# A graph attention layer with gathered rows: other PSUM banks for three intermediate results, masks fetched first, and a clearing behind each gather

## The chip, the cores and the metric

The kernel runs on one core of one Trainium2 chip. The metric is the device time of one execution in microseconds (us); the median of several runs is what counts. Engines are named as in the profile: PE does the matrix products (PEld its weight loads), DVE is the vector engine, ACT the scalar engine, POOL is GpSimd, SP the engine that here only starts transfers. PSUM is the memory that PE writes to, divided into banks; SBUF is the memory that all engines share.

## The reference

There are 3125 nodes with 128 features (`x`), and 100000 edges with a source, a destination and one of five types. The edges are sorted by destination. For each type r, and eight heads of 16 features:

```python
mask = edge_types == r
q = jnp.einsum('eh,khd->ekd', x_dst, W_Q[r])
k = jnp.einsum('eh,khd->ekd', x_src, W_K[r])
v = jnp.einsum('eh,khd->ekd', x_src, W_V[r])
logits = (q * k).sum(-1) / scale + attn_bias[r][None, :]
masked_logits = jnp.where(mask[:, None], logits, NEG)
max_v = jax.ops.segment_max(masked_logits, dst, num_segments=n)
max_v = jnp.maximum(max_v, NEG)
exp_l = jnp.where(mask[:, None], jnp.exp(masked_logits - max_v[dst]), 0.0)
sum_exp = jax.ops.segment_sum(exp_l, dst, num_segments=n)
attn = exp_l / (sum_exp[dst] + 1e-12)
out = out + jax.ops.segment_sum(attn[:, :, None] * v, dst, num_segments=n)
```

So it is a softmax over the edges of one type that end in one node, and a weighted sum of values. The sum over types is projected, `x` is added and a layer norm taken; the kernel's output is the layer norm of `x` plus that.

## The kernel before

The edges are cut into 196 groups of 512 (`GE`), a group into 4 tiles of 128 (`T`). They are worked off in 66 steps (`NST`): the first has one group, all others three, so twelve tiles.

*Prologue.* Up to about 132 us the kernel multiplies all nodes with the weights of all types and stores rows of keys and values in a table in device memory (`kv_d`, from the lines 522 and 525), prepares keys and masks of the edges and the first blocks of query rows (`q_d`), and checks its input. Its SBUF tiles are given back (`pre.close()`), and the pool `flow`, from which the loop takes its tiles, lies in that space.

*Gathers.* Each tile of 128 edges needs 128 rows of the table. `gather` (line 865) fetches them by an indirect transfer that POOL starts, one for each tile, 719 in all. They go into four places that are used in turn, two in `kv_early` and two in `kv_late`. `point(k, j, leave)` stands at eleven places of a step; each lets the gathers go that are due by then, two steps ahead (`KV_LEAD`), behind the instruction `leave` (`behind`, line 150, adds that as a wait). One tile of each of 63 steps is not gathered but computed (the "early" tile): `early_places` makes a 0/1 matrix on ACT (lines 1046, 1047), `early_turn` selects columns of `x` with it on PE (1052, into `lt`), `early_turned` copies them to `xr` on ACT (1056), `early_rows` multiplies them with the weights on PE (1063), and `early_keep` copies the rows to their place on ACT (1070).

*One step k*, in the order of the program (`for k in range(NST)`; each engine runs its own instructions in this order, and waits where data or a bank is not free):

- places of one group on ACT (1132, 1136): 0/1 matrices that later sum edges into nodes;
- `products` on DVE (958): queries, spread to the edges, times gathered keys; `logits` (999) sums them over the features of a head into `spare`; `closed_lanes` (973) adds a mask of types; `turn_logits` (1031) transposes them on PE into `lt`;
- `norm` of step k-2 on DVE (1168 to 1172), `relations` (1188, PE: the sum over types, called rows by node) and `by_node` (1192, ACT: copies them to their place among the nodes);
- `spread_q` on PE (938): spreads the queries of step k+1 to its edges, into `qe`; `queries` (896, PE) and `first_part`, `remainder`, `second_part`, `third_part` (901 to 914, ACT and DVE) make query rows of later blocks, in three parts of bf16, and `store_q` stores them;
- `weigh` of step k-1 on DVE (1119): values times weights; `sums` on PE (1146, 1151) for the three groups of step k-1, into `both`, with other work between;
- `scans` on DVE (1076, 1079): the running maximum within a node, from `lt` and masks (`mk`) that a transfer brought; `less_max` (1088, DVE), `exps` (1096, ACT), `turn_exps` (1103, PE, into `mid`), `weights` (1113, ACT, a copy out of `mid`);
- `take(k)` on SP: starts the transfers for later steps, first the keys (`fetch_keys`, 741) and twelve sets of query rows (`fetch_rows`, 764), then the masks (`fetch_masks`, 924).

Blocks of 128 nodes that are complete are projected, normed and stored between these (`project` and others).

*PSUM.* Eight banks are in use: `mid` (one bank), `qe` (three), `lt` (two), `both` (one) and one under the tag `fin`. Waits between engines arise by bank within a tile: an instruction that writes a bank waits for those that still read it. Before the change, `mid` holds the weights of the edges, `spare`, and what is projected; `qe` is taken anew for spread queries and for the rows of the x tile in turn; `both` holds sums, denominators and the rows by node; `fin` holds query rows.

Of the kernel before, what the change touches and what calls it, by code (L numbers as in the profile page):

```python
# [18 lines left out]
P = 128  # L19
# [123 lines left out]
def windowed_path(  # L143
# [684 lines left out]
    ps = ctx.enter_context(tc.tile_pool(name="ps", bufs=1, space=PSUM))  # L828
    late = kv_tile("kv_late", KVB - KVA)
    mid = ps.tile([P, 4 * P], F32, name="mid")  # L830
    flow = ctx.enter_context(tc.tile_pool(name="flow", bufs=2))

    def place(k):
# [23 lines left out]
        for k in range(NST)  # L857
    ]
    issued = []

    def gather(leave=None, n=1):
        for q in sum(tiles, [])[len(issued) :][: max(n, 0)]:
            ((kv, at, _),) = runs(q, q + 1)
            behind(
                nc.gpsimd.indirect_dma_start(  # L865
                    out=kv[:, at, :], out_offset=None, in_=kv_d[:, :],
                    in_offset=bass.IndirectOffsetOnAxis(
                        ap=idx[:, q % T, q // T : q // T + 1], axis=0
                    ),
                ),  # L870
                leave,
            )
            issued.append(q)

    def point(k, j, leave):
        at = k + (j + 1) / POINTS + KV_LEAD
# [15 lines left out]
    def queries(b, c0, c1):  # L892
        if c0 == 0:
            live["q3", b] = flow.tile([P, R, 3, H], BF16, name="q3", bufs=2)
        pr = ps.tile([P, c1 - c0, H], F32, name="prq", tag="fin")
        nc.tensor.matmul(pr, live["xT", b], wq[:, c0:c1, :], start=True, stop=True)  # L896
        live["pr", b, c0] = pr, live["q3", b][:, c0:c1], c1 - c0

# [21 lines left out]
    def fetch_masks(k):  # L920
        n = len(groups(k))
        live["mk", k] = mk = flow.tile([L3, MW], BF16, name="mk", bufs=2)
        rows = msk_d[G0[k] : G0[k] + n]
        nc.sync.dma_start(
            mk[: n * LANES, :],
            bass.AP(tensor=rows.tensor, offset=rows.offset, ap=[[MW, n], [0, LANES], [1, MW]]),
        )

    def spread_q(k):
        hot, qw = live.pop(("hot", k)), live.pop(("qw", k))  # L930
        n = B0[k + 1] - B0[k]
        live["qe", k] = qe = ps.tile([P, T * G3, H], F32, name="qe")
        dest = [qe[:, j, :] for j in range(min(n, T * G3))]
        if k == 0:
            live["qe0"] = qe0 = ps.tile([P, H], F32, name="qe0", tag="fin")
            dest = [qe0] + dest
        for j in range(n):
            spread = nc.tensor.matmul(  # L938
                dest[j], hot[:, j * P : (j + 1) * P], qw[:, j, :], start=True, stop=True
            )  # L940
        return spread
# [3 lines left out]

    def products(k):
        a, b = B0[k], B0[k + 1]
        qe = live.pop(("qe", k))
        if k == 0:
            ((kv, c0, c1),) = runs(0, 1)  # L950
            nc.vector.tensor_tensor(
                kv[:, c0, :H], kv[:, c0, :H], live.pop("qe0"), op=ALU.mult
            )
            a = 1
        n = 0
        for kv, c0, c1 in runs(a, b):
            m = n + c1 - c0
            made = nc.vector.tensor_tensor(
                kv[:, c0:c1, :H], kv[:, c0:c1, :H], qe[:, n:m], op=ALU.mult
            )  # L960
            n = m
        return made
# [3 lines left out]
            live["lx", k] = flow.tile([P, T * (G3 + 1), R, HEADS], F32, name="lx", bufs=2)  # L966
        return live["lx", k]

    spare = mid[:, 2 * P : 2 * P + (T * G3 + 1) * HEADS].rearrange("p (t k) -> p t k", k=HEADS)

    def closed(a, lg, q0):
        n, m = lg.shape[1], a.shape[1]
# [84 lines left out]

    def early_rows(k):
        xr = live.pop("xr")
        qe = ps.tile([P, T * G3, H], F32, name="qe")  # L1060
        live["rows"] = rows = qe[:, :2, :].rearrange("p s h -> p (s h)")
        for r in range(R):
            nc.tensor.matmul(  # L1063
                rows, xr[:, r * P : (r + 1) * P], wkv[:, r].rearrange("h s c -> h (s c)"),
                start=(r == 0), stop=(r == R - 1),
            )

    def early_keep(k):
        ((kv, c0, _),) = runs(B0[k + 1] - 1, B0[k + 1])
        nc.scalar.copy(kv[:, c0, :], live.pop("rows"))  # L1070
# [86 lines left out]
    def both(k):  # L1157
        if ("both", k) not in live:
            live["both", k] = ps.tile([P, G3 * (PW + HEADS + WN)], F32, name="both")
        return live["both", k]  # L1160
# [18 lines left out]
        live.pop(("both", k))  # L1179
        return begun, ended  # L1180

    def relations(k, room=None):
        o5 = live.pop(("o5", k))
        if room is None:
            room = both(k + 1)[:, G3 * (PW + HEADS) :]
        live["nodes", k] = nodes = room[:, : G3 * WN].rearrange("p (g w) -> p g w", g=G3)
        for i, g in enumerate(groups(k)):
            nc.tensor.matmul(nodes[:, i], o5[:, i], rsum[:WR], start=True, stop=True)  # L1188
# [150 lines left out]
    fetch_rows(2)  # L1339

    def take(k):
        if k + 3 < NST:
            fetch_keys(k + 3)
            fetch_rows(k + 3)
        if k + 2 < NST:
            fetch_masks(k + 2)

    def half(k):
        if k - 1 in q_at:
# [4 lines left out]
    for k in range(NST):  # L1354
        new, old = k >= 1, k >= 2
        q0, (q, c0, c1), (q1, d0, _) = q_at.get(k), half(k), half(k - 1)
        done, rooted = block_at.get(k), block_at.get(k - 1)
        place_g, sum_g = list(groups(k - 1)), list(groups(k - 1))

        def place_next():  # L1360
            return places(place_g.pop(0)) if place_g else None

        def sum_next():
            if sum_g:
                sums(sum_g.pop(0))

        soon, near = k + 2 in early_at, k + 1 in early_at
        if q1 is not None:
            second_part(q1, d0)
        if near:  # L1370
            early_turned(lt)
        place_next()
        if soon:
            early_places(k + 2)
        if k == NST - 2:
            places(G0[k + 1])
        elif k == NST - 1:
# [24 lines left out]
        point(k, 0, weigh(k - 1) if new else kept)  # L1402
        point(k, 1, kept)
        pass_on(k)
        if q is not None:
            first_part(q, c0)
        place_next()
        if k == NST - 1:
            place_next()
        sum_next()  # L1410
        for j, leave in enumerate(scans(k)):
            point(k, 2 + j, leave)
        if k == done_at[begun]:
            project(begun)
        if done is not None:
            project(done)
        sum_next()
        lt = live["lt", k]
        less_max(k)
        exps(k)  # L1420
        if q0 is not None:
            turn_q(q0)
            turned(q0)
        placed = place_next() if k < NST - 1 else None
        if k == NST - 1:
            places(G0[k] + 2)
        if k + 2 < NST:
            point(k, 4, spot(k + 2))
        point(k, 5, placed)
        if done is not None:  # L1430
            shifted(done)
            residual(done)
        if k == NST - 1:
            for b in range(NT - len(ends), NT):
                lifted(b)
            for b in range(begun, NT):
                shifted(b)
# [23 lines left out]
    room = ps.tile([P, T * G3, H], F32, name="qe").rearrange("p n h -> p (n h)")  # L1461
    fin = ps.tile([P, RH * H], F32, name="prq", tag="fin")
    live["both", k] = room[:, : G3 * (PW + HEADS + WN)]
    weights(k)
    roots(begun, last=True)
# [540 lines left out]
```

## Time and profile before

| | |
|---|---|
| median of 3 runs | 1312.44 us (1310.02 to 1320.14) |
| the profiled execution's own time | 1318.95 us |
| its span in the trace | 1317.2 us |
| PE / PEld busy | 1006.5 / 743.7 us |
| DVE busy | 904.5 us |
| ACT busy | 689.3 us |
| POOL busy | 797.9 us |
| mean granted clock of PE | 0.838 of full speed |

Times in the trace are microseconds from the span's start. A row of the timeline has the start, the duration, the engine, the line of the kernel, the operation, what is written and read, and in brackets how long the engine had been idle and which instruction ended that. "Remote" stands where the trace names no instruction that ended it, "issue" where the engine waited for nothing that the profile shows. The ends of matrix products are modelled. The chain is followed back from the last instruction, at each step to what released it. For the 719 gathers, the first began at 101.97 us and the last at 1276.74 us.

### The profile page before, as it was taken

How to read it: one execution, taken by the hardware profiler on the slowest of the kernel's cores; microseconds unless marked ns; L12 is line 12 of the kernel's file. 1: busy time of each engine (PE TensorE's matmuls, PEld its weight loads, DVE VectorE, ACT ScalarE, POOL GpSimd, SP SyncE). 2: the span in 40 equal slices, each digit the busy share in tenths (PEclk: the TensorE clock that was granted, in tenths of full speed). 3: DMA queues.
4: the chain of work that ended last, by engine and by line, in shares of the span. 5: the costliest groups of instructions: out<-in, count | busy, mean ns of one | idle time of the engine just before them, and what ended most of it. 6: DMA issues, size and time to landing. Idle time of an engine off the chain costs nothing.

```text
span 1317.2 us, 20087 instructions
## 1 busy us (share of the span) xinstructions
PE 1006.5 (76%) x5425; PEld 743.7 (56%) x5425; DVE 904.5 (69%) x1520; ACT 689.3 (52%) x1882; POOL 797.9 (61%) x793
## 2 busy tenths in 40 slices
PE   6984477988777877878788867777777877787776
PEld 3442355666565655656566655565555656566554
DVE  2545576768775777777776777686677677687776
ACT  1432255656565565546456646455555556465554
POOL 6664566666665666666665756665665566666650
PEclk9996679768888889888788888897888888878877
DMA  6884455555555555545555554555555455555440
GB/s 167 297 292 147 113 141 153 140 150 149 146 142 138 133 148 154 151 129 140 149 137 151 152 148 127 144 136 147 149 146 122 140 152 143 147 150 138 128 107 8
DMA packets 176110, 192.63 MB, mean 146 GB/s; under 512 B 121764, under 2 KB 137072, under 8 KB 175873
## 3 DMA queue, kind: packets, MB, share of 16 engines
q0 software_dynamic: 36528, 98.42, 28.4%
q1 hardware_dynamic: 138271, 91.97, 24.4%
q10 hardware_dynamic: 1194, 0.92, 0.3%
q8 instruction: 44, 0.72, 0.2%
q14 instruction: 73, 0.60, 0.2%
HBM read 160.80 MB, written 30.40 MB: 145 GB/s over the span
## 4 chain that ended last, share of the span: by engine, by line
PE 50%; DVE 16%; ACT 12%; another core or an unknown queue 11%; issue 9%; DMA 1%; SPq 1%; DVEq 0%; ACTq 0%
PE both L1151 14%; PE qe L1063 7%; PE lt L1052 5%; PE pr L522 5%; PE mid L1103 4%; ACT at L1132 4%; PE qe L938 3%; PE both L1146 3%; PE prq L896 2%; PE both L1188 2%; DVE wv L1119 2%; DVE mid L999 2%; DVE run L1076 2%; DVE run L1079 2%
## 5 line engine op out<-in xcount | busy, mean ns | idle before, releaser
L865 POOL DMA_INDIRECT kv_early<-kv_d,idx x366 | 372.2, 1017 | 217.6 <-issue 83.6
L865 POOL DMA_INDIRECT kv_late<-kv_d,idx x353 | 360.2, 1020 | 230.8 <-issue 70.0
L1151 PE MATMUL both<-wv,at 128*125 128x136 f32 x1544 | 326.3, 346 | 57.8 <-ACT oT L1192 24.8
L1151 PEld LDWEIGHTS both<-wv,at 128*125 128x125 f32 x1544 | 257.0, 230 | 142.9 <-issue 70.5
L1132 ACT ACTIVATE at<-wide_at,nkey 128x125 f32<-128x125 f32 x772 | 244.0, 391 | 0.0
L1063 PE MATMUL qe<-wkv,xr 128*128 128x256 f32 x630 | 162.4, 408 | 42.1 <-ACT xr L1056 24.7
L1076 DVE TENSOR_TENSOR_SCAN run<-mk,lt 120x640 f32<-120x640 bf16 (+1 forms) x66 | 97.8, 1482 | 105.6 <-remote 66.1
L1063 PEld LDWEIGHTS qe<-wkv,xr 128*128 128x128 f32 x630 | 124.0, 205 | 63.9 <-ACT xr L1056 27.9
L938 PE MATMUL qe<-qw,hot 120*128 120x128 bf16 x784 | 71.5, 257 | 76.8 <-ACT kv_late L1070 27.9
L1136 ACT ACTIVATE at<-at 128x500 f32<-128x500 f32 x193 | 119.6, 620 | 6.1
L938 PEld LDWEIGHTS <-hot 120*128 120x128 bf16 x784 | 66.7, 124 | 79.0 <-issue 78.4
L1188 PE MATMUL both<-rsum,o 125*128 125x25 f32 x380 | 59.7, 291 | 56.2 <-DVE o L1172 42.4
L1079 DVE TENSOR_TENSOR_SCAN run<-mk,run 120x640 f32<-120x640 bf16 (+1 forms) x66 | 98.5, 1492 | 2.3
L1052 PE MATMUL lt<-diag,xg 128*128 128x512 f32 x252 | 98.6, 520 | 0.0
L1103 PE MATMUL mid<-gather_heads,ls 120*128 120x24 f32 (+1 forms) x528 | 75.5, 283 | 22.6 <-ACT xTq L890 12.6
L999 DVE TENSOR_REDUCE mid<-kv_early 128x8 f32<-128x128 f32 (+3 forms) x51 | 61.3, 1202 | 45.6 <-ACT wv L1113 31.8
L1192 ACT COPY oT<-both 128x25 f32 x190 | 34.2, 180 | 111.4 <-PE both L1188 33.3
L1103 PEld LDWEIGHTS mid<-gather_heads,ls 120*128 120x128 f32 (+1 forms) x528 | 73.7, 215 | 29.6 <-ACT xTq L890 15.4
L1188 PEld LDWEIGHTS both<-rsum,o 125*128 125x128 f32 x380 | 53.6, 213 | 61.8 <-issue 56.5
L1146 PE MATMUL both<-wv,over 128*5 128x136 f32 x384 | 87.8, 316 | 0.0
L999 DVE TENSOR_REDUCE mid<-kv_late 128x8 f32<-128x128 f32 (+2 forms) x48 | 58.9, 1227 | 39.5 <-ACT wv L1113 29.1
L1168 DVE TENSOR_SCALAR both<-both 125x24 f32<-125x24 f32 (+1 forms) x65 | 12.1, 186 | 101.7 <-remote 49.2
(205 smaller groups left out, 1475.1 us busy)
## 6 DMA issues: line engine op xcount, KB each, us to landing
qw<-q_d SPq DMA_DIRECT2D x784, 30.0 KB
kt<-key_d SPq DMA_DIRECT2D x64, 360.0 KB
kv_d<-kvs SPq DMA_DIRECT2D x24, 640.0 KB
q_d<-q SPq DMA_DIRECT2D x25, 480.0 KB
mk<-msk_d SPq DMA_DIRECT2D x65, 150.2 KB
kv_early<-kv_d,idx POOLq DMA_INDIRECT x366
kv_late<-kv_d,idx POOLq DMA_INDIRECT x353
out<-z SPq DMA_DIRECT2D x24, 64.0 KB
```

The source lines that it names most:

```text
L865: nc.gpsimd.indirect_dma_start(out=kv[:, at, :], out_offset=None, in_=kv_d[:, :], in_offset=bass.IndirectOffsetOnAxis(ap=idx[:, q % T, q / ...
L938: spread = nc.tensor.matmul(dest[j], hot[:, j * P : (j + 1) * P], qw[:, j, :], start=True, stop=True)
L999: made = nc.vector.tensor_reduce(lg[:, n : n + c1 - c0], heads(kv[:, c0:c1, :H]), AX.X, ALU.add)
L1052: nc.tensor.matmul(lt[:, c0:c1], xg[:, e, :], at[:, c0:c1], start=True, stop=True)
L1063: nc.tensor.matmul(rows, xr[:, r * P : (r + 1) * P], wkv[:, r].rearrange("h s c -> h (s c)"), start=(r == 0), stop=(r == R - 1),)
L1076: there = nc.vector.tensor_tensor_scan(run[:n], mk[:n, :WIDE], lt, -BIG, op0=ALU.add, op1=ALU.max)
L1079: back = nc.vector.tensor_tensor_scan(run[:n, ::-1], mk[:n, WIDE:0:-1], run[:n, ::-1], -BIG, op0=ALU.add, op1=ALU.max)
L1103: nc.tensor.matmul(ex.rearrange("p (i t) k -> p t i k", t=T)[:, t], ls[: n * LANES, t * P : (t + 1) * P], gather_heads[: n * LANES, :n], s ...
L1132: nc.scalar.activation(at[:, t, :], row_at[:, :WR], AF.Abs, bias=nkey[:, t, g : g + 1], scale=1.0)
L1146: nc.tensor.matmul(pp[:R], over[:, g, :], live["wv", last][:, T * j + T - 1, :], start=False, stop=False,)
L1151: nc.tensor.matmul(pp[:WR], at[:, t, :], wv[:, T * i + t, :], start=(t == 0), stop=(t == end))
L1188: nc.tensor.matmul(nodes[:, i], o5[:, i], rsum[:WR], start=True, stop=True)
```

## The change

It has four parts.

1. *Banks.* `qe` (three banks) and `fin` (one) become tiles that are allocated once, as `mid` is. The sums over heads (`spare`) go from `mid` to the third bank of `qe`, behind the spread queries. The rows of the x tile (`early_rows`) go from a fresh `qe` to `mid`. The rows by node (`relations`) go from `both` to the end of `fin`, where the query rows are too.
2. *Order.* `early_rows` and `early_keep` stand right behind the first placement, ahead of `early_places` and the products. `third_part` and `store_q` stand ahead of `norm`. `queries` and `first_part` stand behind the first sums.
3. *Masks.* `take` starts the masks' transfer ahead of keys and query rows.
4. *Clearing.* A tile `idle` of 128 x 128 float32, which nothing reads, is taken from `flow`, and POOL clears it behind each gather. Beside it, the space reserved for the descriptors of such transfers is set to 8192 bytes.

```diff
     mid = ps.tile([P, 4 * P], F32, name="mid")
+    qe = ps.tile([P, T * G3, H], F32, name="qe")
+    fin = ps.tile([P, 4 * P], F32, name="fin")
...
+    idle = flow.tile([P, P], F32, name="idle", bufs=1)
...
             issued.append(q)
+            nc.gpsimd.memset(idle, 0.0)
...
-        pr = ps.tile([P, c1 - c0, H], F32, name="prq", tag="fin")
+        pr = fin[:, : (c1 - c0) * H].rearrange("p (c h) -> p c h", h=H)
...
-        live["qe", k] = qe = ps.tile([P, T * G3, H], F32, name="qe")
...
-    spare = mid[:, 2 * P : 2 * P + (T * G3 + 1) * HEADS].rearrange("p (t k) -> p t k", k=HEADS)
+    spare = qe[:, 2 * T, : (T * G3 + 1) * HEADS].rearrange("p (t k) -> p t k", k=HEADS)
...
-        qe = ps.tile([P, T * G3, H], F32, name="qe")
-        live["rows"] = rows = qe[:, :2, :].rearrange("p s h -> p (s h)")
+        live["rows"] = rows = mid[:, P : 3 * P]
...
-    def relations(k, room=None):
+    def relations(k, room):
         o5 = live.pop(("o5", k))
-        if room is None:
-            room = both(k + 1)[:, G3 * (PW + HEADS) :]
...
     def take(k):
+        if k + 2 < NST:
+            fetch_masks(k + 2)
         if k + 3 < NST:
             fetch_keys(k + 3)
             fetch_rows(k + 3)
-        if k + 2 < NST:
-            fetch_masks(k + 2)
...
         place_next()
+        if near:
+            early_rows(k + 1)
+            early_keep(k + 1)
         if soon:
             early_places(k + 2)
...
-        if near:
-            early_rows(k + 1)
-            early_keep(k + 1)
         point(k - 1, 8, logits(k))
...
-        if old:
-            for j, leave in enumerate(norm(k - 2)):
-                point(k - 1, 9 + j, leave)
-            relations(k - 2)
-            by_node(k - 2)
-        if k + 1 < NST:
-            kept = spread_q(k + 1)
         if q1 is not None:
             third_part(q1, d0)
             if d0:
                 store_q(q1)
-        if q is not None:
-            queries(q, c0, c1)
+        if old:
+            for j, leave in enumerate(norm(k - 2)):
+                point(k - 1, 9 + j, leave)
+            relations(k - 2, fin[:, 3 * P :])
+            by_node(k - 2)
+        if k + 1 < NST:
+            kept = spread_q(k + 1)
         point(k, 0, weigh(k - 1) if new else kept)
...
-        if q is not None:
-            first_part(q, c0)
         place_next()
...
         sum_next()
+        if q is not None:
+            queries(q, c0, c1)
+            first_part(q, c0)
...
-    nc = bacc.Bacc("TRN2", target_bir_lowering=False, num_devices=1)
+    nc = bacc.Bacc("TRN2", target_bir_lowering=False, num_devices=1, dynamic_dma_scratch_size=8192)
```

More of the change, by code (lines that the diff above doesn't have):

```diff
@@ L931, in spread_q @@
         n = B0[k + 1] - B0[k]
-        live["qe", k] = qe = ps.tile([P, T * G3, H], F32, name="qe")
         dest = [qe[:, j, :] for j in range(min(n, T * G3))]
         if k == 0:
-            live["qe0"] = qe0 = ps.tile([P, H], F32, name="qe0", tag="fin")
+            live["qe0"] = qe0 = fin[:, :H]
             dest = [qe0] + dest
@@ L947, in products @@
         a, b = B0[k], B0[k + 1]
-        qe = live.pop(("qe", k))
         if k == 0:
@@ L1460, in windowed_path @@
     assert full_at(rest[1]) < G0[k] and len(g) == G3
-    room = ps.tile([P, T * G3, H], F32, name="qe").rearrange("p n h -> p (n h)")
-    fin = ps.tile([P, RH * H], F32, name="prq", tag="fin")
+    room = qe.rearrange("p n h -> p (n h)")
     live["both", k] = room[:, : G3 * (PW + HEADS + WN)]
```

## The prediction

> **What bounds the kernel now.** I read the engine shares first, then the chain, the costliest groups, the table of waits, and one step of the timeline. The first two lines below are the span and the busy times, the third is the chain by engine, then the two groups of gathers (busy us, mean ns | idle before, and what ended most of it).
>
> ```profile
> span 1317.2 us, 20087 instructions
> PE 1006.5 (76%) x5425; PEld 743.7 (56%) x5425; DVE 904.5 (69%) x1520; ACT 689.3 (52%) x1882; POOL 797.9 (61%) x793
> PE 50%; DVE 16%; ACT 12%; another core or an unknown queue 11%; issue 9%; DMA 1%; SPq 1%; DVEq 0%; ACTq 0%
> L865 POOL DMA_INDIRECT kv_early<-kv_d,idx x366 | 372.2, 1017 | 217.6 <-issue 83.6 <-PE qe L938 31.3 <-DVE both L1168 21.1
> L865 POOL DMA_INDIRECT kv_late<-kv_d,idx x353 | 360.2, 1020 | 230.8 <-issue 70.0 <-PE qe L938 31.5 <-DVE both L1168 25.3
> ```
>
> No engine is full. PE carries half of the chain, and 11% of it, 0.11 x 1317.2 = 145 us, is time for which the trace names no producer (there is one core, so "another core" is not the reason). The table of waits says where such time appears (us in total, times, longest):
>
> ```profile
> DVE run L1076 <- remote: 66.1, 17, 10.7
> DVE mid L999 <- ACT wv L1113: 60.9, 25, 6.1
> ACT kv_early L1070 <- remote: 57.2, 13, 7.7
> ACT kv_late L1070 <- remote: 53.0, 11, 6.7
> DVE both L1168 <- remote: 49.2, 15, 4.5
> PE qe L938 <- ACT kv_late L1070: 27.9, 7, 5.9
> PE qe L938 <- ACT kv_early L1070: 25.9, 8, 4.4
> PE both L1151 <- ACT oT L1192: 24.8, 17, 3.2
> ```
>
> The three kinds that wait for "remote" all read what PE has just written: the scan the transposed logits, the copy L1070 the rows of the x tile, L1168 the sums. One step of the timeline (start, us, engine, line) shows what such a wait is:
>
> ```profile
> 646.28 2.32 PE L1063 MATMUL qe<-wkv,xr 128*128 128x256 f32 x10
> 648.44 0.81 PE L1031 MATMUL lt<-ident,lx 128*120 128x128 f32 x6
> 648.61 0.94 POOL L865 DMA_INDIRECT kv_late<-kv_d,idx  x1 [0.30 <-issue]
> 650.00 0.95 POOL L865 DMA_INDIRECT kv_late<-kv_d,idx  x1 [0.45 <-DVE both L1168]
> 650.81 1.00 PE L1188 MATMUL both<-rsum,o 125*128 125x25 f32 x6 [1.56 <-issue]
> 651.25 0.95 POOL L865 DMA_INDIRECT kv_late<-kv_d,idx  x1 [0.30 <-issue]
> 652.59 0.95 POOL L865 DMA_INDIRECT kv_late<-kv_d,idx  x1 [0.40 <-DVE wv L1119]
> 655.35 0.37 ACT L1070 COPY kv_late<-qe 128x256 f32<-128x256 f32 x1 [6.32 <-remote]
> 655.43 1.49 DVE L1076 TENSOR_TENSOR_SCAN run<-mk,lt 120x640 f32<-120x640 bf16 x1 [3.11 <-remote]
> 655.78 1.44 PE L938 MATMUL qe<-qw,hot 120*128 120x128 bf16 x12 [3.96 <-ACT kv_late L1070]
> 657.49 1.71 POOL L865 DMA_INDIRECT kv_late<-kv_d,idx  x1 [3.95 <-PE qe L938]
> ```
>
> L1063 ends at 648.6 and L1031 at 649.25, yet their readers begin at 655.35 and 655.43, 80 ns apart, 2.8 us after the start of the last of a string of gathers spaced 1.25 to 1.39 us. Then PE, whose queue holds L938 behind that copy, goes on, and so does POOL. My reading is that PE's completions come late while gathers follow one another closely; the two ends are 6.7 and 6.2 us late here. That is an inference from the order of events, not a row that names a cause.
>
> **The parts.** *Start of the loop.* The clearing is one instruction behind each of the 719 gathers. Its tile lies where the prologue's tiles were, so the first clearing waits for the prologue's last vector work, and gathers 2 to 16 (the rows of steps 0 and 1) wait behind it on POOL. Before, they ran under the prologue:
>
> ```profile
> 101.97 0.94 POOL L865 DMA_INDIRECT kv_early<-kv_d,idx  x1 [5.14 <-DMA kt<-key_d]
> ...
> 123.76 0.95 POOL L865 DMA_INDIRECT kv_early<-kv_d,idx  x1 [0.30 <-DVE first L451]
> 140.55 1.77 POOL L865 DMA_INDIRECT kv_late<-kv_d,idx  x1 [15.85 <-DVE run L1076]
> 132.06 0.13 DVE L665 TENSOR_SCALAR vio<-last 1x1 f32<-1x1 f32 x1
> 144.13 1.61 DVE L958 TENSOR_TENSOR kv_early<-kv_early,qe 128x1408 f32<-128x1408 f32 x1
> 159.80 1.49 DVE L1076 TENSOR_TENSOR_SCAN run<-mk,lt 120x640 f32<-120x640 bf16 x1 [10.72 <-remote]
> ```
>
> At a period p of gather and clearing, the 15 late ones are done at 132.2 + 15p: 154 for p = 1.45, 158.6 for 1.76. The products of step 1 stood at 144.13, so they move by 10 to 15 us. Of that, up to 10.72 us may disappear in the wait that the next scan had anyway. Bounds 0 and +15; I take +7, the middle at p = 1.45 being 5, rounded up for the landing of the last rows, which no row gives.
>
> *The period.* A gather takes 0.95 and the next begins 0.30 later: 1.25. The nearest row of the clearing is a constant cleared at the same shape, and the four small ones before it:
>
> ```profile
> 0.26 0.10 POOL L1993 MEMSET const-float32-0.0<- 128x1 f32 x1 [0.26 <-issue]
> 0.29 0.10 POOL L1993 MEMSET const-float32-1.0<- 128x1 f32 x1
> 0.83 0.20 POOL masks.py:197 MEMSET ident<- 128x128 f32 x1 [0.37 <-POOLq L1993]
> 1.11 0.29 POOL masks.py:199 TENSOR_SCALAR_AFFINE_SELECT ident<-ident 128x128 f32<-128x128 f32 x1
> 1276.74 0.95 POOL L865 DMA_INDIRECT kv_early<-kv_d,idx  x1 [0.30 <-issue]
> ```
>
> So it takes 0.20, and its successor may begin 0.03 (small) to 0.28 us after it. If it fits into the 0.30, p stays 1.25; if it comes on top and brings a second gap of 0.30, p = 1.25 + 0.20 + 0.30 = 1.76 (0.204 and 0.305 unrounded). I take its own duration on top, p = 1.45, between these. What that allows: from 132.2, 718 periods, then the 1317.2 - 1276.74 = 40.5 us that follow the last gather, and the 1.75 us between span (1317.2) and the profiled execution's own time (1318.95): T(p) = 174.4 + 718p. That is 1072 for 1.25, 1215 for 1.45, 1319 for 1.594, 1438 for 1.76. At 1.45 POOL keeps about 100 us for its waits for other engines, against 448.4 - 153.6 = 295 us (all idle time of the two groups less "issue") before. So the cover is thinner, but POOL is not yet the bound.
>
> The Trainium skill ("GPSIMD Engine Reference", section 2.1 Instruction dispatch) says that consecutive Pool instructions are no barrier: a core starts the next one when its own share is done. The starts 0.03 us apart of the small clearings agree; by it alone p would be an estimated 1.28 and T(p) 1094, no limit at all. The same page (section 1, Specifications) says that GpSimd shares its SBUF interfaces with VectorE, which collide when a DVE instruction has two SBUF inputs; this speaks against the change. As an estimate, 719 x 0.204 = 147 us of clearing under a DVE that is 69% busy would stretch it by up to 101 us, of which its 16% of the chain would be 16 us, and the sum below 1294 in place of 1278. No row of before has a clearing under DVE work.
>
> *What the clearing does to the held completions.* It puts another kind of instruction between gathers. The bounds are wide: a gain of the whole 145 us of the chain, or a longer string. Eleven gathers of a step take 11 x 1.25 = 13.75 us now and 15.95 at 1.45; if a completion is still held to the end of a string, each hold grows by up to 2.2 us. 24 holds (13 + 11 of L1070) cost 53 us. I take a tenth of the 145 as gain, 15 us: in the step above spacings of 1.34 and 1.39 did not release PE, so I don't count on much of it.
>
> *Banks and order.* Sums over heads leave the bank that ACT's copy L1113 reads, so the wait at L999 (60.9 us) goes. DVE has 16 of the 78 points that engines hold of the chain, a fifth: 12 us. Rows by node leave the bank of the sums, so PE's wait at L1151 (24.8 us) goes; PE has half of the chain: 12 us. The rows of the x tile leave the bank of the spread queries and run earlier, behind the first placement, so L938 no longer waits for L1070 (27.9 + 25.9 = 53.8 us). But in the step above that copy itself waited for PE's held completion, and whatever next reads PE's work, the scan (held to 655.43), is late with it; so only a sixth, 9 us. Together 33. The bounds are 0 (each wait ends on the next held completion) and 139.5 (all of them). New waits stand against it: the products with V wait for the early copy's read of the bank with the rows (0.37 us of ACT, by then some DVE instructions old), and the queries wait for the copies by node, moved behind the first sums. Both have those sums or scans as cover; without it each costs about such a copy's 0.37 us a step. Nothing taken.
>
> *Masks first.* On SP the masks' transfer goes ahead of keys and 12 rows of queries instead of behind them, 12.3 us sooner, and these move back by 0.75 us (a row of the waits of line 1076, and two of the timeline):
>
> ```profile
> DMA mk<-msk_d: 1.3, 1
> ...
> 644.43 12.29 SPq L764 DMA_DIRECT2D qw<-q_d  x12
> 656.77 0.75 SPq L924 DMA_DIRECT2D mk<-msk_d  x1
> ```
>
> One wait of 1.3 us in the whole loop was for masks. Fetched a step ahead, neither they nor the rows set anything: 0.
>
> **The sum**, against the profiled execution's 1318.95: + 7 - 33 - 15 = 1278. The median of the runs shown, 1312.44, is 0.5% below that execution, so in its terms 1278 x 0.995 = 1272. Its own range, 1250 to 1300, takes the banks' gain from a fifth to twice what I took.
>
> **Rivals.** *A, strings broken:* the clearings let PE's completions through at once. For it: PE's readers are never late without gathers in flight in the step shown. Against it: spacings of 1.34 and 1.39 did not help there. Four tenths of 145 on the path, 58 us: 1318.95 + 7 - 33 - 58 = 1235, in the median's terms 1229; T(1.45) = 1215 (1209) is the floor. *B, longer strings:* spacing releases nothing, and every hold ends one longer string later: 1318.95 + 7 - 33 + 53 = 1346, or 1339. It decides from the point where the extra 2.2 us a step outlasts the banks' gain. For it: holds end with the last gather, and POOL's waits are what bounds the strings today. Against it: POOL still has idle time that a step can take. *C, POOL becomes the bound:* p above 1.594, where T(p) passes 1319; at 1.65, 1359, or 1352. For it: 11 x 1.65 = 18.2 us a step is longer than the (1276.74 - 140.55) / 64 = 17.8 that a step took; against it, the clearing's own row of 0.20. *D, it changes nothing that counts:* the waits taken from the banks end on the same held completions, and the clearing fits into the gap: 1319, or 1312.
>
> **Chances.** The forecast 0.38, A 0.17, B 0.20, C 0.13, D 0.12. About 1% (13 us) is what a measurement of this kernel tells from no change, so: faster 0.38 + 0.17 = 0.55, within 1% 0.12, slower 0.20 + 0.13 = 0.33. The range runs from near A's floor, 1212, to C at p = 1.672, T = 1375, or 1368.
>
> **What would show it.** POOL: a clearing row of about 0.2 us and gathers 1.45 apart in a string; 1.6 or more, with "issue" or the clearing as releaser, is C. Start: the second gather after 132 and the products of step 1 at 151 to 156. Banks: no "ACT wv" ahead of the sums over heads, no "ACT oT" ahead of the sums, no early copy ahead of L938's counterpart. Holds: "remote" in sum below 225.5 (66.1 + 57.2 + 53.0 + 49.2) by a tenth under the forecast, by more than half under A, above 225.5 under B. The forecast is wrong if p leaves 1.25 to 1.55, or if the banks' waits vanish while the time between scans stays at 17.8 us or more.

## The result, and the profile after

The changed kernel takes 1357.07 us (median of 4 runs, 1351.62 to 1360.48), the kernel before 1315.95 beside it: a ratio of 1.034, with a 95% interval of 1.030 to 1.038. The forecast was 1272 us, faster, with a range of its own of 1250 to 1300; the time lies above that and on the wrong side, though inside the wide range of all rivals, 1212 to 1368. Some executions of a kernel are disturbed and take some per cent longer: medians below are of all runs, ratios of the undisturbed ones only, so the two can differ a little.

The page of the changed kernel, busy times and chain (lines of the kernel shift by one to three: 868 is the gather, 877 the clearing, 1033 the transposed logits, 1064 and 1071 the rows of the x tile and their copy, 1077 the scan, 1120 the products with V, 1152 the sums, 1169 the denominators):

```profile
span 1355.4 us, 20694 instructions
PE 1026.3 (76%) x5425; PEld 750.4 (55%) x5425; DVE 915.0 (68%) x1520; ACT 692.8 (51%) x1882; POOL 977.6 (72%) x1512
PE 29%; POOL 22%; DVE 17%; issue 14%; another core or an unknown queue 9%; ACT 6%; DMA 3%; SPq 0%; POOLq 0%; ACTq 0%; DVEq 0%
```

No engine is nearer to full than before, except POOL (72% for 61%), yet POOL now has 22% of the chain, where it had no entry (11% in a second profiled execution of the same kernel). Why a POOL with 28% idle time gets there is in the table of waits (rows of it: us in total, times, longest; the last row is from the kernel before):

```profile
PE both L1152 <- DVE wv L1120: 137.2, 45, 6.0
ACT kv_early L1071 <- remote: 88.6, 14, 7.9
DVE wv L1120 <- ACT kv_late L1071: 76.7, 20, 6.6
POOL kv_late L868 <- DVE wv L1120: 68.8, 23, 4.1
ACT kv_late L1071 <- remote: 63.5, 9, 7.9
DVE wv L1120 <- ACT kv_early L1071: 59.6, 16, 5.2
ACT kv_late L1071 <- PE qe L941: 51.0, 9, 7.1
POOL kv_early L868 <- DVE wv L1120: 49.6, 19, 3.5
DVE both L1169 <- remote: 29.8, 9, 4.0
ACT kv_early L1071 <- PE qe L941: 24.4, 4, 6.9
POOL idle L877 <- DVE vio L665: 22.1, 1, 22.1
...
DVE wv L1119 <- ACT wv L1113: 1.6, 1, 1.6
```

The three waits that the banks were to remove, those of the sums over heads, the sums and the spread queries for a copy of ACT, are not among its costly rows any more. In their place is one that was not there. The products with V (before 1.6 us of waits in all) wait 136.3 us for ACT's copy of the rows of the x tile; behind them the sums wait 137.2 us and the gathers 118.4. The copy itself waits 152 us for "remote", against 110 before, and another 75.4 us that the trace puts down to L941, which does not write the bank that the copy reads. So late completions of PE are still there ("hold" below means the time for which one is late). In all 36 waits the products begin 0.03 to 0.04 us after the copy's end, so it is the copy that they wait for, and not only PE's rows. One step of the timeline shows the chain of them:

```profile
663.45 2.32 PE L1064 MATMUL mid<-wkv,xr 128*128 128x256 f32 x10
663.58 0.95 POOL L868 DMA_INDIRECT kv_late<-kv_d,idx  x1 [0.16 <-issue]
...
666.41 0.83 PE L1033 MATMUL lt<-ident,lx 128*120 128x128 f32 x6 [0.64 <-issue]
...
668.94 0.95 POOL L868 DMA_INDIRECT kv_late<-kv_d,idx  x1 [0.17 <-issue]
...
670.28 0.96 POOL L868 DMA_INDIRECT kv_late<-kv_d,idx  x1 [0.17 <-issue]
...
672.57 0.37 ACT L1071 COPY kv_late<-mid 128x256 f32<-128x256 f32 x1 [7.86 <-remote]
...
672.97 1.75 DVE L1120 TENSOR_TENSOR wv<-kv_early,mid 128x1536 f32<-128x1536 f32 x1 [5.04 <-ACT kv_late L1071]
...
674.64 1.48 DVE L1077 TENSOR_TENSOR_SCAN run<-mk,lt 120x640 f32<-120x640 bf16 x1
...
674.87 1.69 PE L1152 MATMUL both<-wv,at 128*125 128x136 f32 x6 [5.02 <-DVE wv L1120]
...
675.81 0.95 POOL L868 DMA_INDIRECT kv_late<-kv_d,idx  x1 [4.34 <-issue]
```

The rows end at 665.8; the copy starts at 672.57, 2.3 us after the start of the last gather of a string. Before, DVE did the products with V during such a hold, and the scan began when it ended; this is the row for it in the step of before, where copy and scan were held to 655.35 and 655.43:

```profile
650.58 1.74 DVE L1119 TENSOR_TENSOR wv<-kv_early,mid 128x1536 f32<-128x1536 f32 x1
```

Now the products stand in the hold too, and after it 1.75 us of products come ahead of the scan, and the sums and the gathers behind `point(k, 0)` come after them.

The clearing itself is cheap on POOL, and its first one is late (rows of POOL's timeline):

```profile
101.81 0.95 POOL L868 DMA_INDIRECT kv_early<-kv_d,idx  x1 [5.99 <-DMA kt<-key_d]
124.81 0.20 POOL L877 MEMSET idle<- 128x128 f32 x1 [22.06 <-DVE vio L665]
...
128.30 0.95 POOL L868 DMA_INDIRECT kv_early<-kv_d,idx  x1 [0.17 <-issue]
129.25 0.22 POOL L877 MEMSET idle<- 128x128 f32 x1
129.64 0.95 POOL L868 DMA_INDIRECT kv_early<-kv_d,idx  x1 [0.17 <-issue]
```

From 128.30 to 129.64 is a period of 1.34 us: the clearing follows the gather at once and takes over part of the gap, which shrinks from 0.30 to 0.17. So 0.22 us of clearing add 0.09 us to the period.

### The profile page after: what moved, and what is told of

Same layout as the page of the kernel before. It is cut to its first block, busy times and chain, and to the rows that moved or that the text cites. A ratio compares the mean times of both kernels' runs of the same rounds, so it can differ in the third digit from the quotient of the medians.

```text
span 1355.4 us, 20694 instructions
## 1 busy us (share of the span) xinstructions
PE 1026.3 (76%) x5425; PEld 750.4 (55%) x5425; DVE 915.0 (68%) x1520; ACT 692.8 (51%) x1882; POOL 977.6 (72%) x1512
## 4 chain that ended last, share of the span: by engine, by line
PE 29%; POOL 22%; DVE 17%; issue 14%; another core or an unknown queue 9%; ACT 6%; DMA 3%; SPq 0%; POOLq 0%; ACTq 0%; DVEq 0%
POOL kv_early L868 9%; POOL kv_late L868 9%; PE both L1152 8%; PE mid L1064 4%; POOL idle L877 4%; PE pr L522 4%; DVE wv L1120 3%; PE lt L1054 3%; DVE run L1080 2%; DVE run L1077 2%; PE mid L1104 2%; PE both L1147 2%; ACT at L1133 2%; DVE qe L1001 2%
## 5 line engine op out<-in xcount | busy, mean ns | idle before, releaser
L868 POOL DMA_INDIRECT kv_early<-kv_d,idx x366 | 384.9, 1052 | 140.9 <-issue 53.2
L1152 PE MATMUL both<-wv,at 128*125 128x136 f32 x1544 | 349.3, 364 | 151.8 <-DVE wv L1120 137.2
L1152 PEld LDWEIGHTS both<-wv,at 128*125 128x125 f32 x1544 | 271.6, 243 | 235.7 <-issue 190.4
L877 POOL MEMSET idle<- 128x128 f32 x719 | 159.2, 221 | 22.5 <-DVE vio L665 22.1
L1064 PE MATMUL mid<-wkv,xr 128*128 128x256 f32 x630 | 156.1, 397 | 24.1 <-ACT xr L1058 15.7
L1064 PEld LDWEIGHTS mid<-wkv,xr 128*128 128x128 f32 x630 | 120.7, 200 | 42.2 <-ACT xr L1058 17.7
L1120 DVE TENSOR_TENSOR wv<-kv_early,mid 128x1536 f32<-128x1536 f32 (+1 forms) x36 | 58.6, 1633 | 86.2 <-ACT kv_late L1071 45.3
L1120 DVE TENSOR_TENSOR wv<-kv_late,mid 128x1536 f32<-128x1536 f32 x32 | 56.1, 1752 | 77.7 <-ACT kv_late L1071 31.4
L1187 PE MATMUL fin<-rsum,o 125*128 125x25 f32 x380 | 58.1, 286 | 58.9 <-DVE o L1173 30.2
L1104 PEld LDWEIGHTS mid<-gather_heads,ls 120*128 120x128 f32 (+1 forms) x528 | 77.6, 225 | 27.3 <-ACT xTq L894 13.4
L1187 PEld LDWEIGHTS fin<-rsum,o 125*128 125x128 f32 x380 | 51.3, 205 | 66.4 <-DVE o L1173 32.4
L1071 ACT COPY kv_late<-mid 128x256 f32<-128x256 f32 x31 | 11.5, 372 | 138.6 <-remote 63.5
```

What stands on the lines that cost most here:

```text
L868: nc.gpsimd.indirect_dma_start(out=kv[:, at, :], out_offset=None, in_=kv_d[:, :], in_offset=bass.IndirectOffsetOnAxis(ap=idx[:, q % T, q / ...
L877: nc.gpsimd.memset(idle, 0.0)
L1064: nc.tensor.matmul(rows, xr[:, r * P : (r + 1) * P], wkv[:, r].rearrange("h s c -> h (s c)"), start=(r == 0), stop=(r == R - 1),)
L1104: nc.tensor.matmul(ex.rearrange("p (i t) k -> p t i k", t=T)[:, t], ls[: n * LANES, t * P : (t + 1) * P], gather_heads[: n * LANES, :n], s ...
L1120: return nc.vector.tensor_tensor(heads(wv[:, a:b, :H]), heads(kv[:, at + a : at + b, H:]), ex[:, a:b, :, None].to_broadcast([P, b - a, HEA ...
L1152: nc.tensor.matmul(pp[:WR], at[:, t, :], wv[:, T * i + t, :], start=(t == 0), stop=(t == end))
```

## The experiments

Theory W: the new wait of the products with V carries the loss. Theory P: the clearing does. Rival O: the other banks or the order do. Ratios are always to the kernel before, run on the same chip in the same set. The sets fell on different chips, and on the first of them something else came out; it is told first.

**First set: a chip on which the kernel before takes 1087 us** (13 runs, 1078.51 to 1089.87). Four kernels: the rows of the x tile put back,

```diff
-        live["rows"] = rows = mid[:, P : 3 * P]
+        live["rows"] = rows = qe[:, :2, :].rearrange("p s h -> p (s h)")
...
-        if near:
-            early_rows(k + 1)
-            early_keep(k + 1)
         if soon:
             early_places(k + 2)
...
         point(k - 1, 7, weighted)
+        if near:
+            early_rows(k + 1)
+            early_keep(k + 1)
```

> The changed kernel with one part undone: the rows of the x tile are again multiplied into qe behind the products, not into mid behind the first placement; the clearing, the other banks, the order and the masks stay. Theory W (the products with V read mid, so they now wait for ACT's copy of those rows out of mid, and that copy waits for a late completion of PE; sums and gathers queue behind them): most of the 136 us that the products with V wait for that copy goes, and with it the loss: about 1300 us, 1285 to 1325. Theory P (the clearing makes each gather's slot longer, 1.34 us in place of 1.25, and POOL gets into the chain): the loss stays, 1345 to 1365.

the clearing and its tile taken out,

```diff
-    idle = flow.tile([P, P], F32, name="idle", bufs=1)
...
-            nc.gpsimd.memset(idle, 0.0)
```

> The changed kernel without the clearing and its tile; banks, order and masks stay. Theory W: the wait of the products with V for the copy stays, over 100 us in sum, and the time stays at 1340 to 1360 (a few us less for the start of the loop). Theory P: the loss goes with the clearing, 1275 to 1320, and the wait of the products with V shrinks to under 50 us.

both,

> Both undone: rows of the x tile back in qe behind the products, no clearing. What is left of the change is the sums over heads in qe, the rows by node in fin, the order and the masks. Theory W and theory P both expect no loss here: W the forecast's gain for these banks, 1280 to 1305; if neither is the cause, and the other banks or the order cost the time, 1340 or more.

and the clearing alone, put into the kernel before (with the 8192 bytes).

> The kernel before with the clearing behind each gather alone (and the smaller space for descriptors that its tile goes with). Theory W: the clearing costs the 2 to 5 us of the start and little more, 1310 to 1330, as gathers 1.34 us apart still leave POOL idle time in each step. Theory P: it carries the whole loss, 1345 to 1365. If the clearing lets PE's completions through (rival A of the prediction), under 1300.

Measured: rows back 1323.61 us (1.221), no clearing 1089.65 (1.006, 1.002 to 1.010), both 1312.40 (1.210), clearing alone 1155.57 (1.065, 1.059 to 1.070). The absolute numbers that were expected don't apply, since they were given for a kernel of 1313 us; that 1323.61 falls into the range of theory W is chance. What the traces of all four show: PE's completions are not late in them. The copy of the rows without the clearing:

```profile
L1069 ACT COPY kv_early<-mid x32: 372/372/373, 139.6 to 1031.4; 128x256 f32<-128x256 f32 x32
L1069 ACT COPY kv_late<-mid x31: 372/372/373, 125.5 to 999.5; 128x256 f32<-128x256 f32 x31
...
  PE mid L1062: 76.1, 63
...
  DVE wv L1118: 18.3, 16
```

Its waits are 76.1 us in 63 steps, all for a PE that is named, none for "remote", and the products with V wait 18.3 us for it instead of 136.3. The banks and the order then cost and bring next to nothing, 0.6%. The clearing costs 6.5% there, because steps are shorter and POOL becomes the bound: 11 slots of 1.34 us are 14.7, and a step took 15.52 us with the clearing alone, 14.55 in the changed kernel without it; 11 times 0.09 us is 0.99, about that difference. POOL leads the chain, and its gathers waited 27.7 us in all for other engines (126.6 us of idle time less "issue"):

```profile
L866 POOL DMA_INDIRECT kv_early<-kv_d,idx x366 | 374.8, 1024 | 65.1 <-issue 51.7 <-DVE run L1078 1.8 <-PE lt L1054 1.5
L866 POOL DMA_INDIRECT kv_late<-kv_d,idx x353 | 355.0, 1006 | 61.5 <-issue 47.2 <-DVE den L1172 1.8 <-DVE stats L1230 1.7
...
POOL 27%; DVE 23%; PE 22%; DMA 13%; issue 8%; ACT 5%; POOLq 0%; SPq 0%; DVEq 0%; ACTq 0%
```

So of the two parts it is the clearing that costs time on this chip, as theory P has it; the whole change was not run there. The rows put back were no undoing. With `spare` now in `qe` beside them, the sums over heads waited for the copy, every step:

```profile
L999 DVE TENSOR_REDUCE qe<-kv_late x48: 295/1628/1761, 125.9 to 1254.5; 128x8 f32<-128x128 f32 x16, 128x96 f32<-128x1536 f32 x16, 128x88 f32<-128x1408 f32 x16
...
  ACT kv_late L1069: 163.2, 31
  ACT kv_early L1069: 141.9, 32
```

305 us of a wait of the same sort as the one under suspicion stand in a kernel of 1312 us in place of 1087, though no completion was late. Not all of the difference need be that wait: PE was also busy longer, 1034.6 us at a granted clock of 0.807, against 923.0 at 0.914 without the clearing on this chip. These two kernels tell nothing about the change, but that one such wait in the middle of a step can go with a large loss.

**Second set: a chip on which the kernel before takes 1309.95 us.** The changed kernel, the two parts once more, and the kernel before with no gathers from the sixth step on (`if q >= T * G0[KVB + 1]: issued.append(q); continue` at the head of the loop in `gather`); it works on with the rows that its places held, so it does not compute the layer.

> The changed kernel itself once more. In the runs of the first experiments the kernel before took 1087 us, not 1313, and PE's completions were hardly ever late. Theory H (late completions belong to the chip of the run, not to the kernel): where before takes about 1087 us, this takes the product of the two parts measured there, 1.006 x 1.065 = 1.07, about 1163 us (1140 to 1185), and the sum of late completions is below 30 us; where before takes about 1313, the ratio is 1.03 again and the sum is above 400 us. Rival (the state belongs to how one kernel happens to lie in memory): before and this fall apart, the ratio is above 1.15.

> The changed kernel without the clearing, once more, beside the changed kernel. On a chip without late completions 1.00 to 1.01 of before again. On one with them: theory W (the new wait of the products with V for the copy of the x tile's rows costs the time) 1.02 to 1.035; theory P (the clearing does) 0.97 to 1.005.

> The kernel before with the clearing alone, once more. Without late completions 1.06 to 1.07 of before again, by POOL's slot of 1.34 in place of 1.25 us. With them: theory W 0.995 to 1.015, theory P 1.025 to 1.04.

> The kernel before without the gathers from the sixth step on: the rows stay what the places held, all other work is done. If gathers hold PE's completions, no late completions are left in the steps, whatever the chip, and the time is bound by PE, DVE and the waits between them: 980 to 1060 us. If the holds have another source, the waits for remote at the scan, the copy of the rows and the denominators stay over 100 us in sum on a chip that has them.

Measured: the changed kernel 1350.68 us, 1.031 (1.022 to 1.040); without the clearing 1333.02, 1.019 (1.009 to 1.029), just below what W expected and above all of P; the clearing alone 1322.39, 1.010 (1.006 to 1.014), as W expected. The two parts add up to 2.9%, the whole has 3.1%. The ratio is again that of the first result, so theory H holds as far as this goes: 1.03 goes with a kernel before of 1310. Its other sign failed: the waits for "remote" of the changed kernel add up to some 268 us, not to over 400. Without gathers the time was 1040.77 us (one run). Line 1073 is the copy there; the rows below its own name what ended its waits (us, times):

```profile
L1073 ACT COPY kv_late<-qe x31: 352/354/373, 152.5 to 960.8; 128x256 f32<-128x256 f32 x31
...
  PE qe L1066: 5.2, 10
  PE both L1191: 3.2, 1
```

It waits for nothing named "remote", on a chip where the kernel with gathers has that wait. So the late completions come with the gathers; this is shown, by one run. What of a gather makes them is not, since POOL's instruction and its transfer were left out together, and the granted clock rose with it, to 0.93 from 0.82 or so. That closeness of the gathers makes them, as the prediction read it, is not shown either: at 1.34 us in place of 1.25 they are as late.

**Third set: a chip on which the kernel before takes 1311.08 us.** The wait is taken away by what makes it: the products with V take the weights from ACT's copy in SBUF and read `mid` no more.

```diff
-        wv, ex = live["wv", k], live["ex", k]
+        wv = live["wv", k]
...
-            ex[:, a:b, :, None].to_broadcast([P, b - a, HEADS, HD]), op=ALU.mult,
+            wv[:, a:b, H:, None].to_broadcast([P, b - a, HEADS, HD]), op=ALU.mult,
```

In the changed kernel without the clearing:

> The changed kernel without the clearing, and the products with V take the weights from wv in SBUF (ACT's copy, there already) in place of mid, so that they read no bank that holds the rows of the x tile and do not wait for ACT's copy of these rows. Nothing is left out of the computation. Where completions come late (before about 1310): theory W 0.98 to 1.003 of before, against 1.019 with the wait, and the wait of the products with V for the copy is gone; rival O (the order or the other banks cost the 1.9%, the wait only shows it): 1.012 to 1.025, with the same time in front of another DVE instruction, the scan or the denominators. Where they don't (before about 1087): 0.995 to 1.005 by both.

With it:

> The same with the clearing kept: the changed kernel without its new wait. Where completions come late: theory W 0.995 to 1.015 of before, about what the clearing alone cost (1.010); rival O 1.025 to 1.035, as the changed kernel. Where they don't: 1.06 to 1.07.

In the kernel before, as a control:

> Control: the kernel before with the weights taken from SBUF. Its products with V hardly waited (1.6 us in all), so both theories say 0.995 to 1.005; if it comes out faster by itself, the first kernel's gain is not the wait's.

And the cleared tile in memory outside the prologue's (`ahead.tile` in place of `flow.tile`):

> The changed kernel with the cleared tile in memory that is not the prologue's, so that the first clearing waits for nothing and the gathers of steps 0 and 1 run under the prologue again. The first scan of three groups stood at 162.2 us in place of 159.8, so 2 to 6 us below the changed kernel by that: 1.026 to 1.029 of before where completions come late, 1.055 to 1.068 where they don't. If the start was worth the +7 of the prediction or more, 1.026 or less, and 1.06 or less.

Measured: 1283.17 us without clearing, 0.980 (0.972 to 0.988); 1295.70 with it, 0.989 (0.981 to 0.996); the control 1295.37, 0.985 (0.977 to 0.994); the early start 1345.39, 1.017 (1.007 to 1.027). The first is what W asks for, and faster than both kernels; the wait is gone from its trace, where the products with V wait 1.4 us in all:

```profile
DVE wv L1118 <- ACT wv L1112: 1.4, 1, 1.4
```

The second came out faster than W expected. The control was to come out the same and did not, so the first kernel's gain is not the wait's alone. The last interval was too wide to decide.

**Fourth set: a chip on which the kernel before takes 1311.74 us.** Now the wait alone, in the kernel before:

```diff
-        nc.scalar.copy(kv[:, c0, :], live.pop("rows"))
+        live["copied"] = nc.scalar.copy(kv[:, c0, :], live.pop("rows"))
...
-        return nc.vector.tensor_tensor(
+        made = nc.vector.tensor_tensor(
...
+        behind(made, live.pop("copied", None))
+        return made
```

> The kernel before with one wait added: the products with V wait for ACT's copy of the rows of the x tile in the same step, as they do in the changed kernel by the shared bank. No bank, order or transfer is changed. Where completions come late: theory W 1.015 to 1.035 of before; rival O (the other banks or the order cost the time) 0.995 to 1.01. Where they don't (before about 1087): 0.995 to 1.01 by both.

> The changed kernel without the clearing, beside the next one on one chip: 1.015 to 1.025 of before again where completions come late, 1.00 to 1.01 where they don't.

> The same without the wait (weights from SBUF): 0.975 to 0.99 of before again where completions come late. Theory W: the gap to the kernel with the wait is at least 2.5%, more than the 1.5% that SBUF weights gave the kernel before; rival O: no more than 1.5 to 2%.

> The changed kernel with the cleared tile outside the prologue's memory, once more: 1.026 to 1.03 of before where completions come late, if the late start costs the 2 to 6 us that the first scans show; 1.02 or less if it costs over 13 us. Where they don't come late: 1.055 to 1.068.

Measured: the wait alone 1340.58 us, 1.019 (1.013 to 1.025); without the clearing 1327.82, 1.009 (1.005 to 1.013), below what was expected; the same without the wait 1290.00, 0.981 (0.975 to 0.986); the early start 1342.61, 1.022 (1.016 to 1.028), between what was expected of a cheap and of a dear start. One added wait, with nothing else changed, costs what the banks and the order cost or more, and its waits are the changed kernel's:

```profile
DVE wv L1119 <- ACT kv_early L1070: 80.2, 21, 7.2
POOL kv_early L865 <- DVE wv L1119: 74.2, 22, 4.3
DVE wv L1119 <- ACT kv_late L1070: 69.7, 16, 7.5
POOL kv_late L865 <- DVE wv L1119: 64.6, 25, 4.3
```

149.9 us in 37 steps, for 136.3 in 36. Taking the wait out brought 2.8% here (1.009 to 0.981) and 3.8% across the second and third set (1.019 to 0.980). The control's gain of 1.5% comes off that, which leaves some 1.3 and 2.3% for the wait, with half a per cent or more of uncertainty in each ratio. The wait alone, at 1.9%, is the direct measure. Both speak for W against O.

## Why the prediction was wrong

Where the time goes is seen from the first scans of two steps, read from the timelines of one execution each (us from the span's start; the last column is the difference over 58 steps). The chip of the first set is left out. These executions lie within 0.6% of their kernel's median, except the one with the early start: at 1325.95 us it was the shortest of its six, and its step need not be typical (the one of the third set had 18.19).

| kernel | scan of step 7 | scan of step 65 | us a step |
|---|---|---|---|
| before | 262.7 | 1291.0 | 17.73 |
| changed, and again | 268.9, 273.2 | 1330.3, 1319.9 | 18.30, 18.05 |
| changed, early start (fourth set) | 264.2 | 1299.0 | 17.84 |
| clearing alone (second set) | 274.2 | 1302.0 | 17.72 |
| no clearing (second, fourth) | 263.3, 265.7 | 1302.8, 1297.8 | 17.92, 17.80 |
| wait alone | 265.7 | 1313.5 | 18.07 |
| weights from SBUF, no clearing (third, fourth) | 262.5, 260.0 | 1256.0, 1260.3 | 17.13, 17.25 |
| weights from SBUF, with clearing | 268.7 | 1267.5 | 17.22 |
| before, weights from SBUF | 262.6 | 1269.5 | 17.36 |

*The new waits: the step that failed.* The prediction named this wait, that of the products with V for the early copy, and put it at "0.37 us of ACT ... Nothing taken". It priced the copy's duration, not its start. In the same paragraph it had just argued that "that copy itself waited for PE's held completion", and used that to cut the gain at L938 to a sixth; it did not carry it over to the products. The cover it named, sums and scans, was itself behind the wait in the order of DVE and PE. What it costs was measured by itself: 1.9%, 25 us of 1311.74, and 18.07 - 17.73 = 0.34 us a step in the two traces. With that the prediction's own last sign of being wrong came true: the banks' waits vanished, and a step stayed above 17.8 us, at 18.05 to 18.30.

*The banks' gain* was taken as 33 us. Without the new wait the other banks, the order and the masks bring 0.980 against the control's 0.985 in the third set, 0.5% or 7 us of 1311.08 with intervals that overlap; the traces give 17.36 less 17.13 to 17.25, times 58, which is 6 to 13 us. So this term was two and a half to five times too large, inside its bounds (0 to 139.5). (The prediction's own range, 1250 to 1300, was to reach twice this term; that gives 1239 in the median's terms, not 1250.) The waits named went away but for a few us; yet the time spent in holds hardly fell: all waits for "remote" are some 330 us, for 350 before. They stand before other instructions, as rival D put it. In the kernel without that wait and without clearing, of the third set:

```profile
DVE both L1167 <- remote: 135.6, 34, 6.9
ACT kv_late L1069 <- remote: 50.2, 12, 7.0
ACT wv L1112 <- remote: 40.4, 9, 5.2
```

DVE now meets the hold at the denominators, 135.6 us for 49.2 before.

*The clearing's effect on the holds* was taken as a gain of 15 us. There is no gain: the clearing alone leaves the step at 17.72 us for 17.73, and the waits for "remote" at scan and copy at 68.9 and 101.2 us, for 66.1 and 110.2. Those at the denominators fell, to 20.3 us from 49.2, but the copies of the rows by node took more than that up, 88.8 us for 13.4 (the last row is from the kernel before), and in all they are 355 us for 350:

```profile
ACT oT L1194 <- remote: 88.8, 18, 6.5
DVE run L1078 <- remote: 68.9, 17, 11.3
ACT kv_late L1072 <- remote: 56.3, 10, 7.8
ACT kv_early L1072 <- remote: 44.9, 9, 7.0
...
ACT oT L1192 <- remote: 13.4, 4, 4.1
```

The longer strings of rival B cost nothing in the steps of that kernel either. The sum of "remote" that the prediction named fell by more than a tenth (181.9 us at copy and denominators in the first table, none worth naming at the scan, for 225.5), but the scan, which now stands behind the products, lost more than the whole difference; that number could not tell the cases apart.

*The period* came out at 1.34 us (1.45 taken, 1.25 to 1.76 as bounds), so T is 174.4 + 718 x 1.34 = 1137 us and rival C was away from its point of 1.594. Its mechanism is seen all the same on the chip of the first set, where the clearing alone took 1155.57 us, near that value. The Trainium skill ("GPSIMD Engine Reference", section 2.1 Instruction dispatch) gave an estimate of 1.28 by its rule that consecutive Pool instructions are no barrier; the overlap is there, 0.13 of the 0.30 us gap, but not whole. The other rule that was taken from the Trainium skill (the same page, section 1, Specifications), the SBUF interfaces shared with VectorE, does next to nothing here: DVE is busy 910.4 us without and 914.3 us with the clearing in the second set, 4 us where the prediction's estimate allowed up to 101.

*The start* was +7 us, a term that was right in mechanism and size. The first clearing waited 22 us for the prologue, and gathers 2 to 16 behind it. By the scan of step 7 the four executions with the clearing in the prologue's memory are at 268.7 to 274.2, mean 271.3, and the eight others at 260.0 to 265.7, mean 263.3: 8 us. In the clearing alone it is the clearing's whole cost where completions are late: 11.5 us behind at step 7, 11.0 at step 65. In the changed kernel it is not. With the early start its ratio was 1.022 instead of 1.031 to 1.034, on other chips, but beside it, without the clearing, 1.009, and these intervals do not meet. So about 1.3% of the clearing remains there although the first one waits for nothing; no run says by what, and the two traces, 17.84 and 17.80 us a step, don't show it.

*Masks first* was not tried alone; no wait for masks is among the changed kernel's costly rows.

*The sum* of the terms as measured is 8 for the start, 6 to 13 off for the banks and 25 for the wait: 20 to 27 us, where the changed kernel lost 41 (1357.07 - 1315.95). The rest, 14 to 21 us, is not accounted for; what the clearing costs in the changed kernel beyond its start would be of that size.

*The chain of cause*, then: a late PE completion, which is there anyway; a copy that waits for it, which before held up only the next PE work; the products with V tied to the copy by a bank that both read; and behind the products the sums, the scan and the gathers. *Left open:* why taking the weights from SBUF gains 1.5% in the kernel before, whose products with V waited for almost nothing (the scan's wait for "remote" is 12.1 us there for 66.1); what in a gather holds PE's completions, and why on some chips alone; what the clearing costs the changed kernel beyond its start. The masks, the order and each bank were not tried one by one, nor the 8192 bytes by themselves.

## What to carry to other kernels

A new wait is priced by when the instruction waited for begins, not by how long it takes; ask what that instruction itself waits for, then what stands behind the new waiter on its engine, and add a wait alone to the kernel before to measure it. It is not only an instruction that writes a bank that waits for its readers: two readers of one PSUM bank can be tied to each other although neither writes, as in the 36 waits here of the products for the copy. So give an early result a bank that no busy engine reads late, or read from a copy that is there anyway. An instruction that is put behind each of many others should not take memory that a previous phase has just left, since the first one waits for that phase and holds its whole queue.

## What the runs showed of the hardware

The same program took 1087 us on one chip and 1310 to 1316 on the others, a larger step than the change itself made where it was run, with mean clocks of PE between 0.918 and 0.936 on the one and 0.838 in the profile of before on another. Each chip was used for one set, so what belongs to the chip and what to that time isn't separated. The clock alone does not mark the chip: the two kernels with the rows put back were granted 0.807 to 0.814 on the first one. There, the traces of all four kernels have no wait for "remote" at all; on the second set's chip, those at the copy go away with the gathers (1041 us, clock 0.93). What a change is worth differs with that: the clearing costs 6.5% on the one kind of chip and 1% on the other, the banks and the order 0.6% and 0.9 to 1.9%.
